# First gates inside the last FP4 products, a seven-product output gate for the first block, and weight sums on GpSimd

## The chip, the cores and the metric

The kernel runs on one core of a Trainium2 chip. The metric is its device time in microseconds; less is better. The core has TensorE (matrix products into PSUM, eight banks), VectorE and ScalarE (elementwise work from SBUF or PSUM), GpSimd (elementwise work from SBUF), SyncE (which issues most DMAs), and each of them works through its own instructions in order. Between engines an instruction waits on semaphores.

## The reference

Two layers over B = 2 sequences of T = 1024 tokens of C = 512 channels, all in float32: linear attention, a feed-forward part with FP4 weights, gated linear attention, and a feed-forward part over the 512 best-scored tokens of each sequence, each with a residual and a layer norm. The change lies at the seam of the second and third part:

```python
y = jnp.einsum('bsi,hi->bsh', h, w_down)                      # end of the FP4 part
y = y / jnp.sqrt(jnp.mean(y * y, axis=-1, keepdims=True) + EPS)
x = layernorm(x + y)
q = jax.nn.softmax(x @ Wq.T, axis=-1)                         # third part: 32 channels each
k = jax.nn.sigmoid(x @ Wk.T)
gf = jax.nn.log_sigmoid(-k)
o = _gla_chunk(q, k, x, gf)                                   # chunks of 64 tokens, decayed state
go = o @ Wog.T + x @ Wig.T                                    # the output gate, 512 x 512 each
on = o * lax.rsqrt(jnp.mean(o * o, axis=-1, keepdims=True) + EPS) * g_norm_w
x = layernorm(x + (on * (go * jax.nn.sigmoid(go))) @ Wo.T)
```

## The kernel before

The 2048 tokens are four blocks of 512; blocks 0 and 1 are the first sequence. The residual stream stays in SBUF (`x_t[blk]`, four tiles of 128 tokens), and its transpose is made on TensorE tile by tile (`turn`, L653, banks named `x2Tp`). A framework assigns the instructions to the engines, sets the waits, and orders each engine's stream; `tc.issue_after(ins)` puts what follows behind `ins` in the order. PSUM banks come in turn from two rings of four, `mm_bank` and `acc_bank`, and a product waits until the bank's last reader is done.

Many large products are made by seven block products instead of eight: sums of blocks of both operands, seven products of half size, and sums of the results.

- **FP4 down products** (`down`, L745 and L754): for each block P1, P2, P5, P4, P6, P7, P3, P8. Sums of their operands, `S` and `h`, are made on GpSimd (L760), the results are added into `y` on VectorE (L766 to L790). For the last block they run at the end of the stage in seven pieces, with the transposes of block 1 (`turn(1, ...)`) and the gate logits of the first sequence, `lp` (L661), between pieces. Then follow on ScalarE the squares of `y` (L823) and on GpSimd the inverse root (L827, L828); `Normed.rest` adds the scaled `y` to `x` on VectorE (L859) and normalises it.
- **`Gates`** (L993 to L1011) turns the logits of one sequence into q, k, l = log of the decay (through Exp and Ln on ScalarE and a reciprocal on VectorE), `ep` (one product with a triangle, L1008), e and kd. Before, it stands behind the FP4 stage.
- **`scores(blk)`** (L1025 to L1077): `cp` and exponentials of it, `tp`, then on VectorE last, km, kk, q4, qm, qk, qi; on TensorE `dp` (L1055), with `decay` copied from it; `sc`, `sk` and the states `up`. For block 0 it takes `fillers`, other work that is put between.
- **`attend(blk)`** (L1094, L1096): products into `op`, copied to `oT` on ScalarE, squares on ScalarE, and their sum `sum2` on GpSimd (L1103); `rms` (L1109) sums it over partitions with `mp`.
- **The output gate**: for blocks 1 to 3 `gate(blk)` (L1156), seven products of 8 matmuls with 256 columns, from sums of weights (`sums_of_gate`, gS1 to gS4 in `gsums`, VectorE, L974 to L977) and sums of x and o (`x_sum`, `o_sum`, `other_sums`, T1, T2, T4). For block 0 `plain_gate` (L1133, L1137): 16 matmuls of 512 columns with `Wig` and 16 with `Wog`, since the sums of weights come later.
- **`finish_by_seven(blk)`** (L1224): the last product with W1o, with sums from `sums_of_W1o` (VectorE, L1201) and `sums_of_u`.

The weights lie in four places, A0 to A3 (`place_w`); a new tenant waits for the last reader of the old one (`uT` takes the place of `y`). `w34` is a pool opened when the FP4 pool `fp4` is closed. `b2` and `rw`, 2 KB per partition each, serve as scratch until their own data is loaded; `rw` is first read at L1276, by the scores of the router for block 0.

Of the kernel before, what the change touches and what calls it, by code (L numbers as in the profile page):

```python
# [10 lines left out]
F32 = mybir.dt.float32  # L11
# [5 lines left out]
ALU = mybir.AluOpType  # L17
# [4 lines left out]
P = 128  # L22
# [51 lines left out]
def body(ctx: ExitStack, tc: tile.TileContext, a: dict, out: bass.AP):  # L74
# [594 lines left out]

    with tc.tile_pool(name="s2", bufs=1) as wk2:  # L670
# [137 lines left out]
        class Normed:  # L808
# [12 lines left out]
            def squares(self, part):  # L821
                for i in part:
                    nc.scalar.activation(junk, self.y[:, i], AF.Square, accum_out=self.ms[:, i : i + 1])  # L823

            def power(self):
                ms = self.ms
                nc.gpsimd.tensor_scalar(ms, ms, 1.0 / C, 1e-6, ALU.mult, ALU.add)  # L827
                nc.gpsimd.tensor_tensor(ms, ms, const("mhalf"), ALU.pow)  # L828
# [26 lines left out]
            def rest(self):  # L855

                for i in range(4):
                    x = x_t[self.blk][:, i]
                    nc.vector.scalar_tensor_tensor(x, self.y[:, i], self.ms[:, i : i + 1], x, ALU.mult, ALU.add)  # L859
                    row_stats(self.mv[:, i], x)  # L860
                    yield
                layernorm(x_t[self.blk], self.mv)
# [61 lines left out]
        for n, steps in enumerate((11, 12, 10, 12, 10, 10, 14)):  # L924
            with tc.issue_after(mm), tc.issue_after(hm):
                take(pieces, steps)
            if n < 2:
                turn(1, (2 * n, 2 * n + 1))
            if n == 2:
                lp = logits(0)  # L930
        now.squares(range(4))
        now.power()
# [8 lines left out]
    w1 = w34.tile([P, KC, DFF], F32, name="w1")  # L941
    nc.sync.dma_start(out=w1, in_=a["w1"].rearrange("(k p) f -> p k f", p=P))
    load_w(W1o, "W1oT")
    nc.sync.dma_start(out=rw, in_=a["rw"].to_broadcast([P, C]))
    nc.sync.dma_start(out=b2, in_=a["b2"].to_broadcast([P, C]))
    jk = ctx.enter_context(tc.tile_pool(name="jk", bufs=2))
    s3 = ctx.enter_context(ExitStack())
    wk = s3.enter_context(tc.tile_pool(name="s3", bufs=1))

    def part(i, shape, name):  # L950

        return w34.tile([P, *shape], F32, tag=f"B{i}", name=name)

# [12 lines left out]
    gsums = [part(i, [2, KC, 256], f"gsums{i}") for i in range(3)]  # L966
# [6 lines left out]
    def sums_of_gate():  # L973
        nc.vector.tensor_add(gS1, gA21, gA22)  # L974
        nc.vector.tensor_sub(gS2, gS1, gA11)
        nc.vector.tensor_sub(gS3, gA11, gA21)
        nc.vector.tensor_sub(gS4, gA12, gS2)  # L977
# [5 lines left out]

    class Gates:


        def __init__(self, lp):
            lg = lp.rearrange("p (i d) -> p i d", d=64)
            q, k, l, e = (wk.tile([P, 8, 32], F32, tag=n, name=n) for n in ("q3", "k3", "l3", "e3"))
            kd = wk.tile([P, 8, 4, 32], F32, tag="kd", name="kd")  # L990
            self.q, self.k, self.l, self.kd = q, k, l, kd

            nc.scalar.activation(k, lg[:, :, 32:], AF.Exp, scale=-1.0)  # L993
            nc.vector.tensor_scalar_add(k, k, 1.0)
            nc.vector.reciprocal(k, k)
            nc.scalar.activation(l, k, AF.Exp)
            nc.scalar.activation(l, l, AF.Ln, bias=const("one"))
            red = sp.tile([P, 8], F32, tag="red", name="red")
            nc.vector.tensor_reduce(red, lg[:, :, :32], AX.X, ALU.max)
            nc.vector.tensor_sub(q, lg[:, :, :32], red.unsqueeze(2).to_broadcast([P, 8, 32]))  # L1000
            nc.scalar.activation(q, q, AF.Exp)
            den = sp.tile([P, 8], F32, tag="den", name="den")
            nc.vector.tensor_reduce(den, q, AX.X, ALU.add)
            nc.vector.reciprocal(den, den)
            nc.vector.tensor_mul(q, q, den.unsqueeze(2).to_broadcast([P, 8, 32]))

            ep = mm_bank("ep")
            nc.tensor.matmul(ep[:, :256], const("suf"), l.rearrange("p i d -> p (i d)"), start=True, stop=True)  # L1008
            nc.scalar.activation(e.rearrange("p i d -> p (i d)"), ep[:, :256], AF.Exp)

            nc.vector.tensor_mul(  # L1011
                kd, e.unsqueeze(2).to_broadcast([P, 8, 4, 32]), k.unsqueeze(2).to_broadcast([P, 8, 4, 32])
            )

    def scores(blk, gates, beside=None):
# [12 lines left out]
        nc.scalar.activation(ex[:, 3], cp[:, :P], AF.Exp, scale=-1.0)  # L1028
# [96 lines left out]
    banks, last_3 = [], [None]  # L1125

    def plain_gate(m, first):

        cut = slice(m * P, (m + 1) * P)
        if first:  # L1130
            banks.append(acc_bank("go"))
            for k in range(KC):
                ins = nc.tensor.matmul(banks[m], Wig[:, k, cut], xT[0][:, k], start=k == 0, stop=False).ins  # L1133
            return ins
        else:
            for k in range(KC):
                nc.tensor.matmul(banks[m], Wog[:, k, cut], oT[0][:, k], start=False, stop=k == KC - 1)  # L1137
            if m == 0:
                uT[0] = place_w(3, "uT")
            sil = wk.tile([P, 512], F32, tag="sil", name="sil", bufs=2)  # L1140
            nc.scalar.activation(sil, banks[m], AF.Silu)
            nc.vector.scalar_tensor_tensor(uT[0][:, m], oT[0][:, m], gw[:, m : m + 1], sil, ALU.mult, ALU.mult)

    def gate(blk):


        u = uT[blk] = uT[0]
        c = u.rearrange("p (m e) (s t) -> p m e s t", e=2, s=2)
        c11, c12, c21, c22 = (c[:, :, e, s] for e in range(2) for s in range(2))
        x = xT[blk]  # L1150

        def product(ps, w, b, half, first):
            with tc.issue_after(last_3[0]):
                for m in range(2):
                    for k in range(KC):
                        ins = nc.tensor.matmul(  # L1156
                            ps[:, 256 * m : 256 * m + 256],
                            w[:, k, m],
                            b[:, k, 256 * half : 256 * half + 256],
                            start=first and m == 0 and k == 0,  # L1160
                            stop=k == KC - 1,
                            skip_group_check=True,
                        ).ins
            last_3[0] = ins
            return ps.rearrange("p (m t) -> p m t", m=2)
# [13 lines left out]
        nc.scalar.copy(c11, product(one, gA11, x, 0, True))  # L1179
        yield  # L1180
        p5 = product(two, gS1, T1, 0, True)
        yield
        nc.scalar.copy(c22, p5)
        yield
        nc.scalar.copy(c12, product(one, gS2, T2, 0, False))
        p2 = product(acc_bank("go"), gA12, oT[blk], 0, True)
        yield nc.vector.tensor_add(c11, c11, p2).ins
        p7 = product(one, gS3, x, 1, False)
        yield nc.vector.tensor_add(c22, c22, p7).ins
        nc.vector.tensor_add(c12, c12, product(two, gS4, oT[blk], 1, False))  # L1190
        yield end(0)
# [4 lines left out]
    def sums_of_W1o():  # L1196
        W1oT = part(3, [4, 512], "W1oT")
        B11, B12, B21, B22 = (W1o.rearrange("p (m e) (o c) -> p m e o c", e=2, o=2)[:, :, e, o] for e in range(2) for o in range(2))
        Ts = [W1oT[:, i].rearrange("p (m c) -> p m c", m=2) for i in range(4)]
        for dst, x, y in ((Ts[0], B12, B11), (Ts[1], B22, Ts[0]), (Ts[3], B21, Ts[1]), (Ts[2], B22, B12)):  # L1200
            nc.vector.tensor_sub(dst, x, y)  # L1201
        return (B11, B21, B22), Ts
# [369 lines left out]
    gates = Gates(lp)  # L1572

    def fillers(h):

        turn(2, (2 * h, 2 * h + 1))
        plain_gate(2 * h, True)
        return plain_gate(2 * h + 1, True)

    scored = scores(0, gates, fillers)  # L1580
    with tc.issue_after(scored):
        for _ in ending:
            pass
        sums_of_gate()
        x_sum(1)
    for blk in range(NB):
        if blk:
            if blk == 1:
                W1o_sums = sums_of_W1o()
            if blk < 3:  # L1590
                sums = sums_of_u()
        sum2 = attend(blk)
        if blk == 0:
            plain_gate(0, False)
        else:
# [13 lines left out]
            next(gating)  # L1609
# [3 lines left out]
        if blk == 1:  # L1613
            turn(3)
            gates = Gates(logits(1))
# [117 lines left out]
```

## Time and profile before

| | us |
|---|---|
| time, median of 3 runs (lowest to highest) | 985.53 (985.15 to 985.74) |
| the profiled execution: time | 985.74 |
| the profiled execution: span in the trace | 983.8 |
| TensorE clock granted, mean | 0.998 |
| last FP4 product P8 issued, first `go` with Wig begins | 551.65 |
| attend(0) begins | 575.77 |
| first product of `finish_by_seven` begins | 611.07 |

A profile line of a group gives line, engine, operation, output and inputs, how many, then busy time and the mean of one. PE is TensorE, DVE VectorE, ACT ScalarE, POOL GpSimd, SP SyncE. A float32 matmul shows as two records. In a timeline the first number is the start in us from the span's begin, the second the duration, and a bracket at the end is the idle time before it with what ended it. In a list of waits the numbers are the total, how many, and the longest.

### The profile page before, as it was taken

To read this page: it belongs to the slowest core of one execution; us is meant where nothing else is said; L and a number is where in the kernel's file an instruction comes from. 1 tells how busy PE (TensorE), PEld (TensorE's weight loads), DVE (VectorE), ACT (ScalarE), POOL (GpSimd) and SP (SyncE) were. 2 spreads that over 40 slices of the span, in tenths; PEclk is the share of its full clock that TensorE was granted. 3 is DMA by queue.
4 is the path that set the end of the run, shared out by engine and by line. 5 is a ranking of instruction groups with operands and counts; after the bars stand their busy time and mean duration, and the time that the engine had idled before them with its cause. 6 is when DMAs were issued, how large, how long until landed. Compare 5 with 4: busy or idle time off the path is not lost. (4 is left out here: it accounts for less than half of the span.)

```text
span 983.8 us, 11753 instructions
## 1 busy us (share of the span) xinstructions
PE 967.1 (98%) x4373; PEld 768.5 (78%) x4373; DVE 697.6 (71%) x1340; ACT 290.3 (30%) x496; POOL 302.9 (31%) x276
## 2 busy tenths in 40 slices
PE   9999999999999999999999999999999999999996
PEld 6668876785888888888889656979768588888885
DVE  3569986987975686686672566565897795789644
ACT  2344323333542272263240442132221123220000
POOL 1110282005887265575565022001032011000022
PEclk9999999999999999999999999999999999999999
DMA  9632222100000000000020500000004302140011
GB/s 333 194 88 74 87 69 64 49 1 1 1 1 1 1 1 1 1 11 1 0 86 1 224 1 1 1 1 1 1 33 139 128 17 70 44 171 1 1 43 43
DMA packets 25979, 48.85 MB, mean 50 GB/s; under 512 B 4684, under 2 KB 6732, under 8 KB 25411
## 3 DMA queue, kind: packets, MB, share of 16 engines
q1 hardware_dynamic: 23283, 42.98, 13.2%
q0 software_dynamic: 1920, 4.22, 1.1%
q10 hardware_dynamic: 720, 0.92, 0.3%
q8 instruction: 34, 0.56, 0.2%
q14 instruction: 22, 0.18, 0.1%
HBM read 39.70 MB, written 10.52 MB: 51 GB/s over the span
## 5 line engine op out<-in xcount | busy, mean ns | idle before, releaser
L181 POOL TENSOR_TENSOR rs<-rs,table 128x4 f32<-128x4 f32 (+1 forms) x21 | 20.3, 967 | 301.3 <-DVE rs L180 301.0
L709 DVE SCALAR_TENSOR_TENSOR gate<-gatep,scale,gate 128x512 f32<-128x512 f32 x123 | 91.5, 744 | 7.4 <-PE gatep L698 6.9
L709 DVE SCALAR_TENSOR_TENSOR up<-upp,scale,up 128x512 f32<-128x512 f32 x112 | 83.2, 743 | 0.2
L698 PE MATMUL gatep<-x1Th,wgu 128*128 128x512 f32 x176 | 73.1, 415 | 0.6 <-DVE x1Tl L212 0.6
L698 PE MATMUL upp<-x1Th,wgu 128*128 128x512 f32 x176 | 70.4, 400 | 0.1
L698 PE MATMUL gatep<-x1Tl,wgu 128*128 128x512 f32 x176 | 69.6, 395 | 0.0
L698 PE MATMUL upp<-x1Tl,wgu 128*128 128x512 f32 x176 | 69.5, 395 | 0.0
L703 ACT ACTIVATE gate<-gatep,scale 128x512 f32<-128x512 f32 x41 | 28.3, 690 | 112.1 <-PE gatep L698 105.7
L745 PE MATMUL P<-wdn,h 128*128 128x256 f32 x256 | 60.5, 379 | 0.0
L898 POOL TENSOR_TENSOR h<-up,gate 128x512 f32<-128x512 f32 x30 | 38.6, 1286 | 69.6 <-ACT gate L897 64.5
L745 PEld LDWEIGHTS P<-wdn,h 128*128 128x128 f32 x256 | 48.5, 190 | 6.7
L1103 POOL TENSOR_TENSOR sum<-sum,sq 128x512 f32<-128x512 f32 x12 | 18.0, 1499 | 101.6 <-issue 77.1
L367 PE MATMUL xk<-pair,x 128*128 128x512 f32 x96 | 42.7, 592 | 0.0
L188 DVE BATCH_NORM_STATS2 st<-x 128x6 f32<-128x512 f32 x64 | 41.9, 677 | 0.4
L698 PEld LDWEIGHTS upp<-x1Th,wgu 128*128 128x128 f32 x176 | 33.0, 188 | 10.6 <-DVE up L709 2.4
L698 PEld LDWEIGHTS gatep<-x1Th,wgu 128*128 128x128 f32 x176 | 33.1, 188 | 8.8 <-DVE gate L709 1.1
L698 PEld LDWEIGHTS upp<-x1Tl,wgu 128*128 128x128 f32 x176 | 33.1, 188 | 7.6 <-issue 0.2
L698 PEld LDWEIGHTS gatep<-x1Tl,wgu 128*128 128x128 f32 x176 | 33.1, 188 | 6.9
L1463 PE MATMUL yp<-w,h 128*128 128x256 f32 x168 | 37.7, 379 | 0.0
L745 PE MATMUL P<-T,S 128*128 128x256 f32 x160 | 35.8, 379 | 0.0
L1463 PEld LDWEIGHTS yp<-w,h 128*128 128x128 f32 x168 | 31.9, 190 | 4.3
L1377 ACT ACTIVATE h<-h,b 128x512 f32<-128x512 f32 x28 | 18.4, 713 | 57.2 <-DVE h L1401 34.6
(459 smaller groups left out, 2325.0 us busy)
## 6 DMA issues: line engine op xcount, KB each, us to landing
pk<-in_gu SPq DMA_DIRECT2D x16, 352.0 KB, 3.8
x<-in_x SPq DMA_DIRECT2D x4, 1024.0 KB, 13.1
w<-in_w SPq DMA_DIRECT2D x1, 4096.0 KB, 14.0
xs<-picked SPq DMA_DIRECT2D x4, 1024.0 KB, 5.1
out<-x SPq DMA_DIRECT2D x4, 1024.0 KB, 4.3
w<-in_w SPq DMA_DIRECT2D x4, 1024.0 KB, 7.0
x0T<-in_xT SPq DMA_DIRECT2D x3, 1024.0 KB, 7.1
pk<-in_dn SPq DMA_DIRECT2D x11, 256.0 KB, 3.4
```

What stands on the lines that cost most here:

```text
L181: power = nc.gpsimd.tensor_tensor(rs[:, :n], rs[:, :n], const("mhalf")[:, :n], ALU.pow).ins
L188: nc.vector.bn_stats(st, x)
L367: ins = nc.tensor.matmul(acc_of[b][c], x_t[blk][:, i, c * P : (c + 1) * P], pairs_of["k", blk][i // 2][:, i % 2], start=blk % 2 == 0 and i ...
L698: ins = nc.tensor.matmul(ps, wgu[:, k, at * P : (at + 1) * P], x[:, k], start=x is parts[0], stop=x is parts[1]).ins
L703: nc.scalar.activation(acc, ps, AF.Copy, scale=s)
L709: last = nc.vector.scalar_tensor_tensor(acc, ps, s, acc, ALU.mult, ALU.add).ins
L745: last_p[0] = nc.tensor.matmul(cut, x(j)[:, r], w[:, j], start=j == 0, stop=j == NP - 1 and tail is None).ins
L898: hm = nc.gpsimd.tensor_mul(h.chunk(f), up, gate).ins
L1103: nc.gpsimd.tensor_add(sum2, sum2, sq)
L1377: nc.scalar.activation(x, x, AF.Gelu_apprx_tanh, bias=b1[:, f : f + 1])
L1463: nc.tensor.matmul(ps[:, 256 * r : 256 * r + 256], x(r, j), w(j), start=j == 0, stop=j == NJ - 1)
```

## The change

- `Gates` moves ahead of the FP4 stage in the code and takes its rooms as an argument; its last step, kd, becomes `decayed`. The first sequence's gates are made behind `lp`, inside the last FP4 products, with q and k in `b2`, l and e in `rw`. The loads of `rw` and `b2` move behind the scores of block 1. For the second sequence it stands where it did.
- Block 0's output gate is made by `gate(0)`, in an order of products of its own; `plain_gate` goes. `x_sum(0)` and the first two products move in among the scores of block 0.
- `sums_of_gate` and `sums_of_W1o` are issued to GpSimd, the first right behind the FP4 stage, the second behind the inverse root of the last block's norm.
- The squares of the last block are issued behind the exponentials of block 0, into a scratch tile of their own, and its norm is split: the additions behind the scores of block 0, the statistics and the norm behind `other_sums(0)`.

```diff
@@ -667,6 +667,38 @@
+    class Gates:
+        def __init__(self, lp, rooms):
+            lg = lp.rearrange("p (i d) -> p i d", d=64)
+            self.q, self.k, self.l, self.e = q, k, l, e = rooms
...
+        def decayed(self, kd):
+            self.kd = kd
+            nc.vector.tensor_mul(
+                kd, self.e.unsqueeze(2).to_broadcast([P, 8, 4, 32]), self.k.unsqueeze(2).to_broadcast([P, 8, 4, 32])
+            )
@@ -857,8 +889,9 @@
                 nc.vector.scalar_tensor_tensor(x, self.y[:, i], self.ms[:, i : i + 1], x, ALU.mult, ALU.add)
-                    row_stats(self.mv[:, i], x)
-                    yield
+                yield
+                for i in range(4):
+                    row_stats(self.mv[:, i], x_t[self.blk][:, i])
                 layernorm(x_t[self.blk], self.mv)
@@ -927,9 +960,10 @@
             if n == 2:
-                lp = logits(0)
-        now.squares(range(4))
-        now.power()
+                gates = Gates(logits(0), [
+                    x[:, i * 256 : (i + 1) * 256].rearrange("p (i d) -> p i d", d=32) for x in (b2, rw) for i in range(2)
+                ])
         ending = now.rest()
@@ -938,18 +972,19 @@
+    gsums = [part(i, [2, KC, 256], f"gsums{i}") for i in range(3)]
+    W1oT = part(3, [4, 512], "W1oT")
     w1 = w34.tile([P, KC, DFF], F32, name="w1")
     nc.sync.dma_start(out=w1, in_=a["w1"].rearrange("(k p) f -> p k f", p=P))
     load_w(W1o, "W1oT")
-    nc.sync.dma_start(out=rw, in_=a["rw"].to_broadcast([P, C]))
-    nc.sync.dma_start(out=b2, in_=a["b2"].to_broadcast([P, C]))
@@ -971,47 +1005,16 @@
     def sums_of_gate():
-        nc.vector.tensor_add(gS1, gA21, gA22)
-        nc.vector.tensor_sub(gS2, gS1, gA11)
-        nc.vector.tensor_sub(gS3, gA11, gA21)
-        nc.vector.tensor_sub(gS4, gA12, gS2)
+        nc.gpsimd.tensor_add(gS1, gA21, gA22)
+        nc.gpsimd.tensor_sub(gS2, gS1, gA11)
+        nc.gpsimd.tensor_sub(gS3, gA11, gA21)
+        nc.gpsimd.tensor_sub(gS4, gA12, gS2)
@@ -1122,35 +1125,15 @@
-    def plain_gate(m, first):
...
     def gate(blk):
-        u = uT[blk] = uT[0]
...
         one, two = acc_bank("go"), acc_bank("go")
-        nc.scalar.copy(c11, product(one, gA11, x, 0, True))
+        p1 = product(one, gA11, x, 0, True)
         yield
         p5 = product(two, gS1, T1, 0, True)
         yield
+        if not uT:
+            uT[0] = place_w(3, "uT")
+        u = uT[blk] = uT[0]
...
+        nc.scalar.copy(c11, p1)
         nc.scalar.copy(c22, p5)
         yield
...
+        if blk == 0:
+            ins = p2()
+            p3 = p3()
+            nc.scalar.copy(c12, product(one, gS2, T2, 0, False))
+            yield ins
+            nc.vector.tensor_add(c12, c12, p3)
+            yield end(0)
+            yield p7()
+        else:
...
     def sums_of_W1o():
-        W1oT = part(3, [4, 512], "W1oT")
...
-            nc.vector.tensor_sub(dst, x, y)
+            nc.gpsimd.tensor_sub(dst, x, y)
@@ -1569,30 +1568,29 @@
-    gates = Gates(lp)
+    new_kd = lambda: wk.tile([P, 8, 4, 32], F32, tag="kd", name="kd")
+    gates.decayed(new_kd())
+    sums_of_gate()
+    x_sum(0)
+    gating = gate(0)
     def fillers(h):
         turn(2, (2 * h, 2 * h + 1))
-        plain_gate(2 * h, True)
-        return plain_gate(2 * h + 1, True)
+        next(gating)
+        return last_3[0]
     scored = scores(0, gates, fillers)
+    with tc.issue_after(last_ex[0]):
+        now.squares(range(4), jk.tile([P, C], F32, tag="junk", name="junk"))
+    powered = now.power()
     with tc.issue_after(scored):
-        for _ in ending:
-            pass
-        sums_of_gate()
-        x_sum(1)
+        next(ending)
     for blk in range(NB):
+        if blk == 1 or blk == 2:
+            sums = sums_of_u()
+        sum2 = attend(blk)
         if blk:
-            if blk == 1:
-                W1o_sums = sums_of_W1o()
-            if blk < 3:
-                sums = sums_of_u()
-        sum2 = attend(blk)
-        if blk == 0:
-            plain_gate(0, False)
-        else:
             o_sum(blk)
...
         if blk == 0:
-            for m in range(1, KC):
-                plain_gate(m, False)
-            continue
+            o_sum(0)
+            with tc.issue_after(powered):
+                W1o_sums = sums_of_W1o()
+            nc.sync.dma_start(out=rw, in_=a["rw"].to_broadcast([P, C]))
+            nc.sync.dma_start(out=b2, in_=a["b2"].to_broadcast([P, C]))
         other_sums(blk)
+        if blk == 0:
+            for _ in ending:
+                pass
```

More of the change, by code (lines that the diff above doesn't have):

```diff
@@ L668, in logits @@
         return lp
+    class Gates:
+        def __init__(self, lp, rooms):
+            lg = lp.rearrange("p (i d) -> p i d", d=64)
+            self.q, self.k, self.l, self.e = q, k, l, e = rooms
+            nc.scalar.activation(k, lg[:, :, 32:], AF.Exp, scale=-1.0)
+            nc.vector.tensor_scalar_add(k, k, 1.0)
+            nc.vector.reciprocal(k, k)
+            nc.scalar.activation(l, k, AF.Exp)
+            nc.scalar.activation(l, l, AF.Ln, bias=const("one"))
+            red = sp.tile([P, 8], F32, tag="red", name="red")
+            nc.vector.tensor_reduce(red, lg[:, :, :32], AX.X, ALU.max)
+            nc.vector.tensor_sub(q, lg[:, :, :32], red.unsqueeze(2).to_broadcast([P, 8, 32]))
+            nc.scalar.activation(q, q, AF.Exp)
+            den = sp.tile([P, 8], F32, tag="den", name="den")
+            nc.vector.tensor_reduce(den, q, AX.X, ALU.add)
+            nc.vector.reciprocal(den, den)
+            nc.vector.tensor_mul(q, q, den.unsqueeze(2).to_broadcast([P, 8, 32]))
+            ep = mm_bank("ep")
+            nc.tensor.matmul(ep[:, :256], const("suf"), l.rearrange("p i d -> p (i d)"), start=True, stop=True)
+            nc.scalar.activation(e.rearrange("p i d -> p (i d)"), ep[:, :256], AF.Exp)
+        def decayed(self, kd):
[3 more added lines that the diff above has]
+            )
     with tc.tile_pool(name="s2", bufs=1) as wk2:
@@ L819, in room, with squares @@
                 return [y[:, s, o] for s in range(2) for o in range(2)]
-            def squares(self, part):
+            def squares(self, part, junk=junk):
                 for i in part:
@@ L827, in power @@
                 nc.gpsimd.tensor_scalar(ms, ms, 1.0 / C, 1e-6, ALU.mult, ALU.add)
-                nc.gpsimd.tensor_tensor(ms, ms, const("mhalf"), ALU.pow)
+                return nc.gpsimd.tensor_tensor(ms, ms, const("mhalf"), ALU.pow).ins
             def scaled(self):
@@ L940, in body, with part @@
     w34 = ctx.enter_context(tc.tile_pool(name="w34", bufs=1))
+    def part(i, shape, name):
+        return w34.tile([P, *shape], F32, tag=f"B{i}", name=name)
+    gsums = [part(i, [2, KC, 256], f"gsums{i}") for i in range(3)]
+    W1oT = part(3, [4, 512], "W1oT")
     w1 = w34.tile([P, KC, DFF], F32, name="w1")
@@ L948, in body @@
     wk = s3.enter_context(tc.tile_pool(name="s3", bufs=1))
-    def part(i, shape, name):
-        return w34.tile([P, *shape], F32, tag=f"B{i}", name=name)
     NJ = NF // 2
@@ L965, in body @@
     )
-    gsums = [part(i, [2, KC, 256], f"gsums{i}") for i in range(3)]
     gS1, gS2, gS4 = (
@@ L982, in body @@
     oT, uT, tri, state, inv = {}, {}, {}, {}, {}
[L984 to L1013, printed above, removed]
     def scores(blk, gates, beside=None):
@@ L1027, in scores @@
         nc.scalar.activation(ex[:, :3].rearrange("p e t -> p (e t)"), cp, AF.Exp)
-        nc.scalar.activation(ex[:, 3], cp[:, :P], AF.Exp, scale=-1.0)
+        last_ex[0] = nc.scalar.activation(ex[:, 3], cp[:, :P], AF.Exp, scale=-1.0).ins
         tp = mm_bank("tp")
@@ L1123, in other_sums @@
         nc.vector.tensor_sub(T4, o[:, :, :256], T2)
-    banks, last_3 = [], [None]
-    def plain_gate(m, first):
[L1129 to L1134, printed above, removed]
-        else:
[L1136 to L1142, printed above, removed]
+    last_3, last_ex = [None], [None]
     def gate(blk):
-        u = uT[blk] = uT[0]
-        c = u.rearrange("p (m e) (s t) -> p m e s t", e=2, s=2)
-        c11, c12, c21, c22 = (c[:, :, e, s] for e in range(2) for s in range(2))
         x = xT[blk]
         def product(ps, w, b, half, first):
-            with tc.issue_after(last_3[0]):
+            with tc.issue_after(last_3[0]) if last_3[0] else contextlib.nullcontext():
                 for m in range(2):
@@ L1182, in gate @@
         yield
+        if not uT:
+            uT[0] = place_w(3, "uT")
+        u = uT[blk] = uT[0]
+        c = u.rearrange("p (m e) (s t) -> p m e s t", e=2, s=2)
+        c11, c12, c21, c22 = (c[:, :, e, s] for e in range(2) for s in range(2))
+        nc.scalar.copy(c11, p1)
         nc.scalar.copy(c22, p5)
         yield
[L1185 to L1191, printed above, removed]
+        p2 = lambda: nc.vector.tensor_add(c11, c11, product(acc_bank("go"), gA12, oT[blk], 0, True)).ins
+        p7 = lambda: nc.vector.tensor_add(c22, c22, product(one, gS3, x, 1, False)).ins
+        p3 = lambda: product(two, gS4, oT[blk], 1, False)
+        if blk == 0:
[7 more added lines that the diff above has]
+        else:
+            nc.scalar.copy(c12, product(one, gS2, T2, 0, False))
+            yield p2()
+            yield p7()
+            nc.vector.tensor_add(c12, c12, p3())
+            yield end(0)
         nc.scalar.activation(c21, product(one, gA22, T4, 0, False), AF.Silu)
@@ L1570, in finish_ffn @@
         next(two)
-    gates = Gates(lp)
+    new_kd = lambda: wk.tile([P, 8, 4, 32], F32, tag="kd", name="kd")
[3 more added lines that the diff above has]
+    gating = gate(0)
     def fillers(h):
         turn(2, (2 * h, 2 * h + 1))
-        plain_gate(2 * h, True)
-        return plain_gate(2 * h + 1, True)
+        next(gating)
+        return last_3[0]
     scored = scores(0, gates, fillers)
+    with tc.issue_after(last_ex[0]):
+        now.squares(range(4), jk.tile([P, C], F32, tag="junk", name="junk"))
+    powered = now.power()
     with tc.issue_after(scored):
-        for _ in ending:
-            pass
-        sums_of_gate()
-        x_sum(1)
+        next(ending)
     for blk in range(NB):
+        if blk == 1 or blk == 2:
+            sums = sums_of_u()
+        sum2 = attend(blk)
         if blk:
-            if blk == 1:
-                W1o_sums = sums_of_W1o()
-            if blk < 3:
-                sums = sums_of_u()
-        sum2 = attend(blk)
-        if blk == 0:
-            plain_gate(0, False)
-        else:
             o_sum(blk)
@@ L1608, in body @@
                     next(gating)
-            next(gating)
+        next(gating)
         if blk == 2:
@@ L1614, in body @@
             turn(3)
-            gates = Gates(logits(1))
+            gates = Gates(logits(1), [wk.tile([P, 8, 32], F32, tag=n, name=n) for n in ("q3", "k3", "l3", "e3")])
+            gates.decayed(new_kd())
         if blk < 3:
```

## The prediction

> **What bounds the kernel now.** I read four views, in this order. The page's first part says whether one engine fills the span:
>
> ```profile
> PE 967.1 (98%) x4373; PEld 768.5 (78%) x4373; DVE 697.6 (71%) x1340; ACT 290.3 (30%) x496; POOL 302.9 (31%) x276
> ```
>
> TensorE is without work for 983.8 - 967.1 = 16.7 us only, and most of that is the start and the tail behind the last matmul. So matmul time removed is time won, and each new gap on TensorE is time lost. The second view, the waits of TensorE from 500 to 680 us, lists the gaps where the change works (total us, times, longest):
>
> ```profile
> PE ep L1008 <- ACT l L997: 1.8, 2, 1.3
> PE dp L1055 <- DVE last L1040: 1.5, 2, 1.2
> PE x2Tp L197 <- ACT e L1009: 0.4, 1, 0.4
> PE mp L1109 <- POOL sum L1103: 0.3, 1, 0.3
> ```
>
> The third, the busy times from the first matmul behind the FP4 products (551.65) to the first product of `finish_by_seven` (611.07), which opens and closes the stretch that changes:
>
> ```profile
> 551.65:611.07 59.42, 56.34 (x246) 33.30 (x244) 40.10 (x71) 26.01 (x45) 11.21 (x9) 1.00 0.23 93
> ```
>
> Counted from issue to issue, the four gaps in it are 1.40 (`ep`), 0.51 (`x2Tp`), 0.45 (`mp`) and 1.31 (`dp`), 3.7 us; the rest, 55.7, is matmuls. The fourth view is the timeline, TensorE for prices and VectorE and GpSimd for what happens when both work (start, duration):
>
> ```profile
> 565.55 5.32 PE L1133 MATMUL go<-x2T,Wig 128*128 128x512 f32 x12
> 570.70 1.02 PE L1060 MATMUL sc<-qm,km 128*128 128x512 f32 x2
> ...
> 674.74 3.62 PE L1156 MATMUL go<-x2T,Wig 128*128 128x256 f32 x16
> 678.19 1.89 PE L1224 MATMUL grow<-W1oT,uS 128*128 128x256 f32 x8
> ...
> 580.25 1.55 POOL L1103 TENSOR_TENSOR sum<-sum,sq 128x512 f32<-128x512 f32 x1 [22.64 <-ACT sq L1102]
> 580.68 1.68 DVE L859 SCALAR_TENSOR_TENSOR x<-y,ms,x 128x512 f32<-128x512 f32 x1
> 583.56 2.30 POOL L1103 TENSOR_TENSOR sum<-sum,sq 128x512 f32<-128x512 f32 x1
> 583.56 1.19 DVE L974 TENSOR_TENSOR gsums<-Wig,Wog 128x1024 f32<-128x1024 f32 x1
> 584.76 2.19 DVE L1115 TENSOR_TENSOR gsums<-x2T 128x1024 f32<-128x1024 f32 x1
> 523.23 1.40 POOL L760 TENSOR_TENSOR S<-S,h 128x256 f32<-128x256 f32 x2 [2.59 <-PE P L745]
> ```
>
> An f32 matmul is two records. Of 512 columns it takes (570.70-565.55)/6 = 0.86 us, of 256 (678.19-674.74)/8 = 0.43. In the last six lines VectorE and GpSimd take turns: L859 alone takes 0.72 and here 1.68, since it stands until the GpSimd sum ends at 581.80; the GpSimd sum of 583.56 stands until L974 ends at 584.75; L1115 (1.2 alone) then stands until that sum ends at 585.86. It is one instruction of each, strictly in turn, and only for VectorE instructions with two SBUF inputs: the `y` additions, which read PSUM, keep their 0.69 while GpSimd runs (524.85).
>
> **What the Trainium skill says.** "GPSIMD Engine Reference", Specifications: GpSimd shares its SBUF interfaces with VectorE, with contention for VectorE instructions in a two-port mode or with two SBUF inputs. The trace agrees, and shows that the wait lasts for the other's whole instruction. The same page, section 3.1, gives 4497 ns for a GpSimd tensor_tensor of 2048 f32 elements; half is 2.25, an estimate. The trace has 0.72 for 256 elements and 1.27 for 512, which extends to 1.27 + 2*0.55 = 2.4 for 1024. "VectorE: DVE Perf Modes", the perf-mode tier table: f32 tensor_tensor runs at the lowest rate, 2293 ns for 2048; here 1.19 for 1024 agrees.
>
> **The change part by part.**
>
> *Seven products.* Out go 32 matmuls of 512 columns (27.5 us), in come 7*8 of 256 (24.2): -3.4 us, all on the path.
>
> *Gates early.* The chain `lp` to `l` ran beside nothing in the old place and cost the `ep` and `x2Tp` gaps. Now it starts when `lp` ends at 531.93, under P4. In the old place `l` was ready 5.28 us after its first activation began (553.75 to 559.03). Here that gives 537.3, and 0.3 more because k+1 meets a GpSimd sum of L760. `ep` stands behind one matmul of P6, at 537.40: a gap of 0.25 (0 to 0.7). The two old gaps go, -1.9. `rw` and `b2` as rooms move their loads behind `cp` and `tp` of block 1, some 581; L1276 reads `rw` at 637.7, so even the 10.2 us that the load took beside w1's is hidden. SP's queue has nothing behind them until the fetch of the routed rows. W1o and w1 are issued as before.
>
> *Sums on GpSimd.* This decides. In the built order the first sum, gS1, waits for the very last FP4 product, P8, because the rooms are freed as a pool. It can't run in GpSimd's idle time from 533.5 on. So four sums of 2.4 us start when VectorE's gate chain starts: kd, T1 (x_sum(0), moved ahead of `last`), last, km, kk, q4, qm, qk, qi, decay. Of these kd, T1, qm, qk and qi have two SBUF inputs. Take t=0 when P8 has been issued: 551.65 + 0.43 for `ep` + 0.25 = 552.33.
> - gS1 0.25 to 2.68; kd, ready at 0.85, stands, then 2.68 to 3.76.
> - gS2 3.76 to 6.04 (2.28 when it stood waiting); T1 6.04 to 7.12; gS3 7.12 to 9.40.
> - last to 7.3, km, kk, q4 to 8.1 (prices of 593.90 to 594.96); qm stands, 9.40 to 9.95; gS4 9.95 to 12.23; qk to 12.5; the 128x4 scaling of ms 0.15; qi to 13.2; decay 13.35.
>
> TensorE: cp 0.65, two tp 0.22, x2Tp 0.44, one go 0.43, x2Tp 0.44, seven go 3.02: 5.20. Then dp waits for `last` until 7.3, a gap of 2.1. dp, x2Tp, one go: 8.3. The last x2Tp takes dp's bank and waits for the copy `decay`: until 13.4, a gap of 5.1. Everything on TensorE is queued behind it. Without turns `decay` would be ready at 5.9 and both gaps nothing. If `last` takes a turn too, it is 14.4; with sums of 2.25 instead of 2.4, 12.9.
>
> *Behind it:* x2Tp 0.44, seven go 3.02, sc 0.95, sk 0.58, four up 3.54: attend(0) begins at 21.9 (its scores found VectorE free) and ends at 28.2 (6.25, as in 575.77 to 582.02). Squares are on ACT, 0.75 each, between x2T copies; hidden. The old 3.45 of Wog matmuls that covered the sums of squares are not there: cp 0.73, tp 0.22 and two go 0.86 reach 30.0, and then `mp` waits for the third sum on GpSimd. ACT has the third square at 29.6 as before plus two copies; GpSimd has first the second sum (28.5 to 29.8), then, new in between, the pow of the layer norm, which gives T2 on VectorE a turn (29.8 to 30.85) and takes 0.9, and then 1.2 for the third: 33.0. A gap of 3.0 (2.0 if T2 and pow fit in, 3.8 if the norm's statistics are late). ms3 stands ahead of km, kk, q4 on VectorE; q4 is at 35.1, `up` asks at 35.8. W1o's sums (4*1.27) run on GpSimd at 14 to 19, when VectorE has no two-input work. c11's copy waits for the last L859-like instruction on `y`, 25.9, and is asked at 26.3.
>
> *The rest to `finish_by_seven`:* mp 0.91, dp 0.21, three up with sc and sk 4.2, the six go left of the third product and 32 of the last four 16.4, attend(1) 7.15: 28.9. Work in all: 27.5 us other than the gate, 24.2 gate = 51.7. With gaps 2.1 + 5.1 + 3.0 the first `grow` is at 61.9, that is 614.2, against 611.07: +3.1. Check by differences: -3.4 work, -3.7 old gaps, +10.45 new gaps = +3.3. Behind it, the one-buffer oT of block 1 lands 2.4 us behind `grow`, T2 and the reads of `grow` are done at 66, the next product on that bank asks at 68.8: covered. From there on the order of TensorE is the same, so the difference stays.
>
> The profiled run took 985.74 for a span of 983.8, 1.9 around it; it was 0.2 above the median 985.53. A span of 986.9 makes 988.8 for that run and 988.6 for the median.
>
> **The rivals.**
> 1. *Forecast, turns at the port as in the trace*: +1.6 to +4.7 (the bounds above), 987.1 to 990.2. Chance 0.70.
> 2. *VectorE keeps its pace* (the other side: faster). The mechanism is the same port, at gS1 to gS4: if a GpSimd sum of 1024 lets VectorE in before it ends, the two gaps of 7.2 go, and the time is 985.5 + 3.1 - 7.2 = 981.4. It decides from the point where the turns cost less than 4.1 of the 7.2. For it: GpSimd's tensor_scalar at 119.23 (3.15 long) let one VectorE instruction through. Against: every tensor_tensor pair of the trace is exclusive. 0.11.
> 3. *Only one place bites*: the `mp` gap hides (sums in time), or the turns cost half. About +0.3, 985.8. For: each has a bound of its own. Against: GpSimd's order has pow ahead of the third sum. 0.13.
> 4. *A further gap*: silu of c11/c12 or c22's sum later than the 0.7 us to spare before the last gate product, or `mp` behind late statistics: 991 to 993. 0.06.
> That the change doesn't do what it says is excluded for the products; for the sums, "on GpSimd" doesn't mean beside the FP4 products, as said.
>
> **How the numbers follow.** The likeliest case gives 988.6. The range takes all of case 1 but its edge and most of 3: 985.0 to 990.4, leaving out 2, 4 and a little, 0.19. 0.2% is 2 us, about what a measurement of this kernel can tell from no change: slower is case 4 and nine tenths of case 1 and a little of 3, 0.71; within is the rest of 3 and the low edge of 1, 0.18; faster is 0.11.
>
> **What would show it.** In the new profile: gate work 3.4 shorter; no gap at `ep` over 0.7; kd and T1 above 2 us each in VectorE's rows and qm, qk, qi stretched; the last x2Tp of block 2 waiting some 5 us for `decay`; `dp` 2 for `last`; `mp` 3 for the GpSimd sum. Short kd and T1 rows beside running GpSimd sums would make the prediction wrong, and so would sums that start before P8 ends.

## The result, and the profile after

The changed kernel takes 994.75 us (median of six runs, 993.07 to 996.11) against 985.49 for the kernel before beside it (985.15 to 985.75): a ratio of 1.0092, 95% interval 1.0082 to 1.0102. It is slower by 9.3 us, where 3.1 were forecast, and outside the range. The profiled run took 994.78 for a span of 992.6.

The page of the changed kernel, the line of engine totals, and the row of the clock granted to TensorE in 40 slices (9 is 90% or more):

```profile
PE 970.6 (98%) x4421; PEld 782.5 (79%) x4421; DVE 703.4 (71%) x1339; ACT 288.5 (29%) x496; POOL 318.2 (32%) x284
...
PEclk9999999999999999999999789999999999999998
```

The same row of the kernel before:

```profile
PEclk9999999999999999999999999999999999999999
```

TensorE is busy 3.5 us longer than before, although 3.4 us of gate products went: some matmuls must have become slower. The clock rows say where. In the kernel before all slices have 9; here two slices have 7 and 8, some 545 to 595 us, just where the change is. (The 8 of the last slice lies behind the last matmul and slows nothing.) That row is in every page and was read too lightly.

The waits of TensorE from 500 to 680 us (total us, times, longest):

```profile
PE dp L1058 <- DVE last L1043: 4.2, 2, 3.9
PE mp L1112 <- POOL sum L1106: 3.0, 1, 3.0
PE x2Tp L197 <- DVE decay L1060: 1.4, 1, 1.4
PE ep L692 <- ACT l L681: 0.5, 1, 0.5
```

The forecast's four waits are there, in the places that it named. Next the timeline, TensorE first (start, duration), then VectorE and GpSimd:

```profile
554.62 3.19 PE L1139 MATMUL go<-x2T,Wig 128*128 128x256 f32 x14
561.72 0.59 PE L1058 MATMUL dp<-last,table 128*128 128x4 f32 x2 [3.91 <-DVE last L1043]
...
565.56 1.12 PE L197 MATMUL x2Tp<-table,x 128*128 128x128 f32 x4 [1.44 <-DVE decay L1060]
566.47 5.15 PE L1139 MATMUL go<-gsums,gsums 128*128 128x256 f32 x14
...
587.65 1.87 PE L1112 MATMUL mp<-table,sum 128*128 128x1 f32 x8 [2.99 <-POOL sum L1106]
...
619.92 1.89 PE L1223 MATMUL grow<-W1o,uT 128*128 128x256 f32 x8
...
553.25 2.89 DVE L698 TENSOR_TENSOR kd<-rw,b 128x1024 f32<-128x1024 f32 x1
556.07 3.37 DVE L1118 TENSOR_TENSOR gsums<-x2T 128x1024 f32<-128x1024 f32 x1
559.36 2.30 DVE L1043 TENSOR_SCALAR last<-table,ex 128x4 f32<-128x4 f32 x1
...
552.69 2.36 POOL L1008 TENSOR_TENSOR gsums<-Wig,Wog 128x1024 f32<-128x1024 f32 x1 [19.06 <-PE P L786]
555.13 3.22 POOL L1009 TENSOR_TENSOR gsums<-gsums,Wig 128x1024 f32<-128x1024 f32 x1
558.32 3.32 POOL L1010 TENSOR_TENSOR Wig<-Wig 128x1024 f32<-128x1024 f32 x1
...
584.44 1.92 POOL L181 TENSOR_TENSOR rs<-rs,table 128x4 f32<-128x4 f32 x1
586.35 1.25 POOL L1106 TENSOR_TENSOR sum<-sum,sq 128x512 f32<-128x512 f32 x1
```

The last two lines are the norm's power and the third sum of squares behind it, for which `mp` waits. Two more things are to be seen. VectorE and GpSimd alternate, each standing until the other's whole instruction is over, so that `last`, 128x4 elements, takes 2.30 us. And fourteen records of the same gate matmul take 3.19 us ahead of the first stop and 5.15 behind the stops. The busy times by stretch say what these have in common. Columns: length, then busy time of PE, PEld, DVE, ACT, POOL, the granted clock, DMA share, GB/s.

```profile
552.45:619.92 67.47, 59.12 (x292) 47.16 (x290) 41.35 (x62) 16.55 (x34) 24.43 (x15) 0.87 0.22 86
556.77:560.18 3.41, 1.03 (x5) 0.57 (x3) 3.41 (x2) 0.76 (x3) 3.41 (x2) 1.00 1.00 416
560.18:563.59 3.41, 1.87 (x8) 1.68 (x8) 3.38 (x5) 0.29 (x1) 3.41 (x2) 0.50 1.01 425
563.59:567.00 3.41, 1.97 (x8) 1.35 (x7) 1.91 (x4) 0.58 (x2) 3.24 (x5) 0.50 0.59 250
567.00:570.42 3.42, 3.42 (x10) 2.70 (x9) 0.00 (x0) 0.30 (x1) 3.34 (x3) 0.50 0.00 0
584.09:587.50 3.41, 0.57 (x3) 0.17 (x1) 1.54 (x3) 0.52 (x2) 3.31 (x3) 1.00 0.49 154
587.50:590.91 3.41, 3.26 (x13) 3.08 (x14) 1.16 (x5) 0.00 (x0) 1.12 (x2) 0.50 0.00 0
590.91:594.32 3.41, 3.41 (x8) 2.35 (x9) 1.62 (x4) 0.00 (x0) 0.00 (x0) 0.50 0.00 0
```

The clock is exactly halved, from 560.18 to 570.42 and from 587.50 to 594.32: three and two stretches of 3.41 us. 587.50 lies eight such stretches behind 560.18, so all changes stand on one grid. Each drop comes at the end of a stretch in which TensorE did little (1.03 and 0.57 us of 3.41).

I call this Theory A: a stop costs its own length and then the half clock behind it. The Trainium skill, "TensorE: Matmul & The Clock Gate", Part 1, states such a gate: TensorE falls to half its clock after an idle window of 3413 ns, is back after a busy one, and the window runs freely. The numbers agree with the length and with the half. They differ in one point: neither stretch ahead of a drop was wholly idle, so a stop shorter than the window is enough; here the measurement decides. The experiments set Theory A against two others. Theory B was that the matmuls are slow because of GpSimd's and VectorE's traffic at their shared port, and Theory C that the stops cost only themselves.

### The profile page after: what moved, and what is told of

The parts are those of the page before. It is cut to its first block, busy times and chain, and to the rows that moved or that the text cites. A ratio compares the mean times of both kernels' runs of the same rounds, so it can differ in the third digit from the quotient of the medians.

```text
span 992.6 us, 11851 instructions
## 1 busy us (share of the span) xinstructions
PE 970.6 (98%) x4421; PEld 782.5 (79%) x4421; DVE 703.4 (71%) x1339; ACT 288.5 (29%) x496; POOL 318.2 (32%) x284
```

## The experiments

**Stops without GpSimd (a single run, 1042.19 us against 985.84).** Artificial stops in the kernel before, in a stage where GpSimd's gate sums have no part:

```diff
+    def hold(n):
+        t = jk.tile([P, C], F32, tag="junk", name="hold")
+        nc.scalar.copy(t, last_ps[0])
+        for _ in range(n):
+            nc.scalar.copy(t, t)
+        spot = either_bank("hold")
+        with tc.issue_after(last_hp[0]):
+            held[0] = nc.tensor.matmul(spot[:, :4], ident, t[:, :4], start=True, stop=True).ins
...
     ins = nc.vector.tensor_sub(c21, c21, product(wA22, g, T4)).ins
+    hold(((0, 2, 4, 6), (3, 5, 8, 4))[b][g])
```

The next products are issued behind `held[0]`, so TensorE stands until the copies are done.

> The kernel before, with work added and none left out: behind each of the eight groups of the last layer's first weight, ScalarE copies one product's bank 1 + n times (about 0.55 us each) and a matmul of 4 columns waits for the last copy, so that TensorE stands still 0.9, 1.9, 2.9, 3.9 us in block 0 and 2.4, 3.4, 4.9, 2.9 us in block 1 (estimates). Neither GpSimd nor the port it shares with VectorE has a part in it. Theory A (long gaps halve TensorE's clock): gaps below about 2.5 us leave the clock of the windows at 1.00; those of 3.9 and 4.9 are followed by 3.4 to 7 us at 0.50, and so is 3.4 or 2.9 if it falls badly; the time grows by the gaps, some 23 us, plus 1.7 to 3.5 us for each that halves it, in all 29 to 37 us: 1015 to 1023. Theory B (traffic of GpSimd and the port made the matmuls slow): the clock stays at 1.00 behind every gap, and the time grows by the gaps alone, 1008.5.

The stops came out longer than estimated, 3.25 to 7.56 us (35.9 in all; the eighth was hidden), because the copies came late: the first stood until a subtraction on VectorE was done (793.77 us), and in the second group ScalarE's activations came between them. Each of the seven is followed by half clock: once 3.41 us, five times 6.83, once 10.24. The times by stretch around the first and second stop:

```profile
792.27:795.68 3.41, 1.19 (x6) 1.09 (x7) 3.41 (x8) 1.81 (x2) 0.00 (x0) 1.00 0.00 0
795.68:799.10 3.42, 3.42 (x10) 2.71 (x9) 3.42 (x10) 3.09 (x6) 0.00 (x0) 0.50 0.00 0
799.10:812.75 13.65, 9.66 (x45) 8.17 (x43) 12.76 (x35) 3.74 (x7) 5.04 (x5) 1.00 0.11 39
812.75:819.58 6.83, 6.45 (x16) 5.29 (x17) 0.00 (x0) 0.91 (x2) 3.19 (x4) 0.50 0.21 80
```

In the first pair GpSimd does nothing at all (POOL 0.00) and the clock is 0.50 all the same. Theory B has no place here; Theory C, which is 18 us short in the sum, has none either. The sum closes: 35.9 of stops; 47.8 us of half clock, of which in 11.3 TensorE still stood, so half of the rest, 18.2, lost; eight holding matmuls of some 0.3: 56.5, and 56.35 was measured.

**How short may a stop be (a single run each, 1035.79 and 999.68).** The same edit with the copies begun two products earlier, first with n from 6 to 10, then from 1 to 6:

> The kernel before with work added and none left out, as in the run with holds, but ScalarE's copies begin two products earlier, so that TensorE stands still for less: some 0.5, 1.1, 1.7 and 2.3 us in the four groups of block 0 and 1.1, 1.7, 2.3 and 2.9 in block 1 (estimates, from 0.62 a copy and 1.73 a product). So far a stop of 1.4 left the clock at 1.00 and one of 3.16, 2.3 of it within one stretch of 3.41 us between two possible changes of the clock, halved it. Theory A with a fixed grid of 3.41 us: stops up to 1.4 leave the clock; 2.9 halves it; of those between, the ones with most of their length within one stretch of the grid do, others don't, so equal stops can differ. Time 985.8 + 14 of stops + 2 for the holding matmuls + 1.7 or 3.4 for each that halves: 1003 to 1011. Theory F (each stop costs in proportion to its length): the half-clock time grows smoothly from the shortest stop on.

> The kernel before with work added and none left out: the run with short holds again with fewer copies, since the stops came out at 3.2 to 6.1 us there (3.24 for seven copies and 0.62 to 1.1 more for each further one). Expected stops: about 1.4, 2.0, 2.0 and once 2.6 us, one of some 3 in the first group. Theory A with a fixed grid of 3.41 us: those of 1.4 leave the clock at 1.00; of those of 2.0 and 2.6 some halve it for one stretch of 3.41 us (1.7 us lost each), depending on where they fall in the grid. Time 985.9 + 13 of stops + 2 + 2 to 7: 1003 to 1008. Theory F (in proportion to the length): every stop is followed by some half-clock time, shorter for shorter stops.

The first try missed its sizes: its stops were 3.22 to 6.14 us, and all seven halved the clock, the ones of 3.22 and 3.26 for one stretch, the others for two. The second has the short ones, shorter than estimated too (6.9 us in all where 13 were expected), so its time lies below its range of 1003 to 1008. Its times by stretch, around a stop of 0.52, one of 2.21 and one of 0.95:

```profile
791.43:800.00 8.57, 8.57 (x41) 7.59 (x42) 8.57 (x23) 4.28 (x6) 0.00 (x0) 1.00 0.00 0
803.85:806.21 2.36, 0.15 (x2) 0.00 (x1) 2.36 (x11) 2.21 (x4) 0.05 (x1) 1.00 0.01 3
806.88:810.30 3.42, 3.42 (x10) 2.70 (x9) 3.38 (x7) 1.82 (x3) 2.50 (x4) 0.50 0.21 77
...
821.43:829.00 7.57, 7.57 (x36) 6.72 (x37) 1.51 (x3) 2.38 (x4) 0.00 (x0) 1.00 0.17 48
```

Stops of 0.19, 0.52, 0.95 and 0.95 left the clock alone; 2.21 and 2.09 halved it for one stretch each, 1.7 us lost. So it is a step and not a share of the length, and Theory F is out.

**The stops filled (997.67, then 991.76 with a ratio of 1.0055, 1.0039 to 1.0072).** If the half clock comes from idleness, useless matmuls in the stops must make the kernel faster. The first try, four matmuls ahead of `dp` and three ahead of the last `x2Tp`:

```diff
+    def keep_busy(n, behind_):
+        with tc.issue_after(behind_):
+            for _ in range(n):
+                ins = nc.tensor.matmul(warm[0], ident, x_t[0][:, 0], start=True, stop=True).ins
+        return ins
...
+            return keep_busy(4, last_3[0])
...
+        turn(2, (2,))
+        with tc.issue_after(keep_busy(3, last_turned[0])):
+            turn(2, (3,))
```

> The kernel after with seven idle matmuls of 512 columns added, which nobody reads: four ahead of dp, three ahead of the last x2Tp, 6.0 us put into gaps of 4.1 and some 2.5. TensorE's order is otherwise that of the kernel after, and VectorE and GpSimd do the same. Theory A: the clock stays at 1.00 from 552 to 584, decay is as late as before, and what comes behind it runs at full rate, 2.4 us less: 992.4 (991.5 to 993.3), with more work. Theory B: the gates' products and x2Tp behind the gaps still take twice as long, 994.8 or a little above. What happens at mp stays as it is in both.

This took 997.67 (ratio 1.0120, 1.0104 to 1.0137). The first of the two `x2Tp` in this order is the one that takes dp's bank, so the three added matmuls came behind the wait for `decay` instead of into it; that stop (2.92 us) remained, the clock fell at 565.0 and the added work lay on the path. The second try gives dp's bank to the `x2Tp` that comes last:

```diff
+        banks = [mm_bank("x2Tp") for _ in range(2)]
+        turn(2, (3,), lambda _: banks[1])
+        with tc.issue_after(keep_busy(3, last_turned[0])):
+            turn(2, (2,), lambda _: banks[0])
```

> The kernel after with seven idle matmuls of 512 columns added, which nobody reads, now with the last three behind the x2Tp that doesn't wait for decay and ahead of the one that does. One gate product matmul comes behind decay that stood ahead of it. Theory A: the clock stays at 1.00 from 552 to 584, decay is ready as late as in the kernel after (13.1 us behind the last FP4 product), and sc is issued 17.0 us behind that product in place of 19.0: 2.0 less, 992.7 (992 to 993.6), although TensorE has 6.0 us more to do. Theory B: the matmuls behind decay still take twice as long: 994.8 to 995.5.

Its timeline of TensorE, and its time for the stretch of the first place:

```profile
557.63 3.60 PE L1597 MATMUL warm<-x,table 128*128 128x512 f32 x8
561.70 0.39 PE L1058 MATMUL dp<-last,table 128*128 128x4 f32 x2 [0.48 <-DVE last L1043]
...
565.55 0.66 PE L197 MATMUL x2Tp<-table,x 128*128 128x128 f32 x4 [0.39 <-DVE decay L1060]
566.04 3.62 PE L1139 MATMUL go<-gsums,gsums 128*128 128x256 f32 x16
569.50 1.02 PE L1063 MATMUL sc<-qm,km 128*128 128x512 f32 x2
```

```profile
551.50:584.00 32.50, 30.34 (x150) 21.12 (x148) 24.98 (x33) 11.18 (x26) 21.78 (x13) 1.00 0.43 171
```

`dp` and `x2Tp` are as late as in the changed kernel (9.27 and 13.1 us behind the last FP4 product), GpSimd and VectorE work as there, TensorE has 6 us more to do, and `sc` comes at 17.07 in place of 19.0: sixteen gate records take 3.62 where fourteen took 5.15. That is what Theory A says. The median of the four runs, 991.76, lies 0.24 us below its range and the profiled run, 992.95, inside it; all four lie below Theory B's 994.8.

**The second place (989.17, ratio 1.003, 1.0019 to 1.0040).** `mp` of block 0 issued later:

```diff
-        rms(blk, sum2)
+        if blk:
+            rms(blk, sum2)
+        else:
+            sum2_0 = sum2
...
         for n, done in enumerate(gating):
+            if blk == 0 and n == 0:
+                with tc.issue_after(last_3[0]), tc.issue_after(done):
+                    rms(0, sum2_0)
```

> The kernel after, with mp of block 0 issued behind the gate products that need oT, so that TensorE no longer stands 3 us for the third sum of squares. Theory A: the gap of 3.0 goes and with it the 3.4 us that 6.8 us at half clock cost, 994.75 - 6.4 = 988.3 (987.5 to 989.5). Theory C (the gap costs its own length only and the slow matmuls have another cause): 991.7. Theory D (this place is covered by something later, attend of block 1): 994 to 995.

5.6 us went, for a stop of 3.16 us. In the place of the second stop and its half clock the clock is now 1.00:

```profile
584.09:594.00 9.91, 9.22 (x35) 5.60 (x34) 9.88 (x18) 1.20 (x4) 4.09 (x3) 1.00 0.16 53
```

A stop of 0.69 at `dp` took part of the place. Theory C's 991.7 is out of the range of the runs (988.3 to 989.65).

**The first place: whose sums (986.48, ratio 1.0011, 1.0002 to 1.0020).** The gate's four sums back on VectorE, here the first, the others alike:

```diff
-        nc.gpsimd.tensor_add(gS1, gA21, gA22)
+        nc.vector.tensor_add(gS1, gA21, gA22)
```

> The kernel after, with the four sums of the gate's weights on VectorE in place of GpSimd and nothing else. VectorE has 4 x 1.2 more to do, but no turns; in TensorE's order 13 us of work now stand ahead of what waits for last and decay. Theory A (turns make the gaps, the gaps halve the clock): dp and x2Tp wait 0 to 1.5 us, no half clock there, mp's gap of 3 and its half clock stay: 994.75 - 4.1 - 1.4 - 3.6 + up to 1.5 = 985.7 to 987.2. Theory C: 989 to 990.5. Theory E (VectorE's whole chain is the limit, so the sums cost the same on either engine): 993 to 996.

8.3 us went, inside Theory A's 985.7 to 987.2. Giving VectorE 4.8 us more to do made it ready earlier: kd to gS4 run from 553.11 to 560.00 at 1.22 each, and `dp` waits 0.95, `x2Tp` not at all. The stop at `mp` remains, with one stretch of half clock behind it where the changed kernel has two and the expectation left both. So some 1.6 of the 8.3 us come from there and not from the edit's own place, and the hit is in that part luck; smaller stops at `up` and `sk` (0.70 and 0.17) took some of it back.

**Shorter turns (990.90, ratio 1.0044, 1.0028 to 1.0061).** The sums stay on GpSimd, each cut into four, again the first for all:

```diff
-        nc.gpsimd.tensor_add(gS1, gA21, gA22)
+        for k in range(KC):
+            nc.gpsimd.tensor_add(gS1[:, k], gA21[:, k], gA22[:, k])
```

> The kernel after with each of the four sums of the gate's weights on GpSimd cut into four instructions of 256 elements; nothing else. Theory A with turns of one instruction each: a VectorE instruction now waits 0.7 for its turn in place of 2.3, last is ready at 4.6 us behind the last FP4 product in place of 8.9, decay at 5.8 in place of 13.1, so TensorE (which asks at 5.2 and 6.3) stands at dp and x2Tp 0 to 1.0 in all, and the clock stays at 1.00 there: 994.75 - 4.1 - 1.4 - 3.6 + (0 to 1) = 985.7 to 986.7, mp's stop and its half clock still in it. Theory G (what VectorE loses depends on GpSimd's work as a whole, not on the length of its instructions): as after, 993 to 996.

The first place behaved as Theory A says: VectorE waits less, and the clock stays at 1.00 there. Its timeline on VectorE:

```profile
553.18 1.25 DVE L698 TENSOR_TENSOR kd<-rw,b 128x1024 f32<-128x1024 f32 x1
554.36 1.75 DVE L1122 TENSOR_TENSOR gsums<-x2T 128x1024 f32<-128x1024 f32 x1
556.03 0.69 DVE L1047 TENSOR_SCALAR last<-table,ex 128x4 f32<-128x4 f32 x1
...
570.90 5.42 DVE L891 SCALAR_TENSOR_TENSOR x<-y,ms,x 128x512 f32<-128x512 f32 x4
```

kd takes 1.25 in place of 2.89 and `last` 0.69 in place of 2.30. The miss of 4 us has two parts. My sum had `decay` ahead of qm, qk and qi on VectorE; in this kernel it comes behind them, at 560.54, so `x2Tp` still stood 1.96. And the turns moved on: W1o's sums on GpSimd now met the additions to x (L891, 5.42 for four, 2.73 in the run with sums on VectorE), which held back copies and squares on ScalarE; `tp` waited 2.1, `mp` 3.4, and the clock was halved for three stretches, 10.24 us.

**Both repairs (981.90, ratio 0.9958, 0.9942 to 0.9975; again 981.26, 0.9954, 0.9941 to 0.9968).** Sums on VectorE and `mp` late, the two edits above together:

> Both repairs: the four sums on VectorE, and mp of block 0 behind the gate products that need oT. Theory A, from the two single runs: 986.48 less mp's stop of 3.0 and the 1.7 to 3.4 of its half clock, plus 0 to 0.7 for dp of block 1: 980.1 to 982.5, faster than the kernel before by 3 to 5. If the two are not independent (VectorE late in both places): 984 to 986.

> The two repairs again (the four sums on VectorE, mp of block 0 late), beside the former kernel on one chip: 981.9 (981.5 to 982.5), with a spread below 1 us, since its longest stop is 0.95. Whichever of the two is lower, both stay below the kernel before by 3.5 to 6.

This version is faster than both kernels. Page and waits (500 to 680 us) of the second run:

```profile
PE 963.2 (98%) x4421; PEld 776.4 (79%) x4421; DVE 704.2 (72%) x1343; ACT 288.4 (29%) x496; POOL 308.6 (31%) x280
...
PEclk9999999999999999999999999999999999999998
```

```profile
PE dp L1058 <- DVE last L1043: 1.9, 3, 0.9
PE up L1075 <- DVE A L1067: 0.7, 1, 0.7
...
```

No stop is over 1 us, the clock row is all 9 but for the last slice, and TensorE is busy 3.9 us less than before: the 3.4 of the products that the change saves arrive at last. The second time lies 0.24 us below its expected range, and its spread of 1.2 us missed the 1 us expected.

**Split sums with the repairs (985.08, ratio 0.9991, 0.9984 to 0.9998; then 986.19, 1.0005, 0.9996 to 1.0013).** Two tries to keep the gate's sums on GpSimd, with `mp` late and W1o's sums moved. The second try also puts them behind the last of `other_sums(0)`, and takes a bank that nobody uses:

```diff
+            with tc.issue_after(normed), tc.issue_after(summed), tc.issue_after(last_sum[0]):
+                W1o_sums = sums_of_W1o()
...
+        if h:
+            mm_bank("spare")
```

> The split sums on GpSimd, with mp of block 0 behind the gate products that need oT, and with the sums of W1o on GpSimd behind the last sum of squares of block 0, so that they don't take turns with the additions to x. Theory A, from the run with split sums: 990.9 less 2.1 (tp's wait for squares that came late), 3.4 (mp's stop) and 5.1 (10.24 us at half clock), plus 0.7 for dp of block 1 and up to 1.5 for turns in the new place of W1o's sums: 980.3 to 982.5. If tp's wait has another cause than those turns: 982.4 to 984.6.

> The run with split sums and late mp, with its three remaining stops addressed: a bank left unused so that x2Tp doesn't wait for decay (a stop of 1.96, behind which the clock was halved for 3.41 us in that profile), and W1o's sums on GpSimd behind the last of the gate's input sums of block 0, so that qm, qk and qi of block 1 don't take turns with them (stops of 1.2 and 0.3 at up and sk). Theory A: 985.08 less 1.96, 1.7, 1.2 and 0.3 = 979.9 (979 to 981), and a narrow spread of the repeated times, as the kernel before has, since no stop over 1.4 us is left whose place in the grid could decide; the kernels with such stops spread by 1.8 to 3.8 us. If VectorE's chain ends as late without the decay wait (sc or the first up waits in its place): 982 to 983.5.

Both missed. In the first try the stop of 1.96 at `x2Tp`, harmless for the clock in the run with split sums, halved it for 3.41 us. Their times by stretch, one fence for each kernel, the run with split sums first:

```profile
556.56:559.97 3.41, 2.22 (x14) 1.69 (x12) 3.38 (x7) 1.50 (x5) 3.41 (x5) 1.00 1.02 411
559.97:563.38 3.41, 2.64 (x14) 2.40 (x15) 0.72 (x2) 0.59 (x1) 3.41 (x6) 1.00 1.01 428
```

```profile
557.78:561.19 3.41, 1.46 (x11) 1.05 (x9) 2.67 (x4) 0.58 (x1) 3.41 (x5) 1.00 0.97 406
561.19:564.60 3.41, 3.41 (x9) 2.70 (x9) 0.00 (x0) 0.58 (x1) 3.41 (x6) 0.50 1.01 430
```

An edge of the grid (559.97) cuts the same stop in two in one run and not in the other. W1o's sums then met qm, qk and qi of block 1 (stops of 1.17 and 0.31 at up and sk), which I had allowed for with up to 1.5. The rest of this miss is an error of the sum: the 5.1 us for 10.24 at half clock counted part of the stop at `mp` twice, since only 7.5 of the 10.24 were work, which makes 3.8. In the second try the first place is clean: `sc` 9.69 us behind the last FP4 product, against 13.56. But `issue_after` gives an order and no wait, W1o's sums began at 577.35, and there they met T2 and `last` of block 1:

```profile
577.60 2.28 DVE L1125 TENSOR_TENSOR gsums<-oT,gsums 128x1024 f32<-128x1024 f32 x1
579.80 1.22 DVE L1047 TENSOR_SCALAR last<-table,ex 128x4 f32<-128x4 f32 x1
```

This stop is the second miss: `dp` of block 1 stood 4.76 us and the clock was halved for 6.83. That try therefore doesn't test whether a kernel without such stops spreads less.

## Why the prediction was wrong

Its direction, its four places and their causes were right; the sum missed one term. By its own steps, from the last FP4 product's issue (552.45) to the first `grow` (619.92), 67.5 us where the prediction had 61.9:

- *The stops.* It had 2.1 (`dp`), 5.1 (`x2Tp`) and 3.0 (`mp`). Measured from issue to issue they are 4.08, 1.65 and 3.16. `last` did take a turn at the port, which the prediction had as its other bound, and so the wait moved from `x2Tp` to `dp`; `decay` released `x2Tp` at 13.1 us, 13.4 predicted. That these are so close is in part luck: `last` is missing in the prediction's list of instructions that take a turn, qk (0.41) stands in its sum for a turn that it didn't take, and the two misses cancel. With the short work between the two at full clock, the stop at `x2Tp` would have been 2.8, and the three 10.0 in all, against 10.2. The mechanism (whole turns at the port; the pow ahead of the third sum) and its size were right: the runs with VectorE's sums and with late `mp` took away what they should at the place that they changed, the run with split sums all but a stop of 1.96. That the third sum comes behind the pow is read from the timeline; no run changed that order.
- *The step that failed* is "With gaps 2.1 + 5.1 + 3.0 the first `grow` is at 61.9": each stop was counted at its own length, with all matmuls behind it at the prices of a trace without long stops. The term left out is the half clock. From 565.56 to 570.42 and from 587.65 to 594.32 it lost (4.86 + 6.67)/2 = 5.8 us, and 61.9 + 5.8 - 0.2 = 67.5. Filling the first place, moving the second, and stops in a kernel without the change show it. Between the matmuls of the kernel before no stop was over 1.40 and the clock stayed at 1.00, so no price of its trace held the term. But the trace held the sign: its last matmul ends at 975.4, and from 980.0 on the clock is 0.50, with nothing left to slow.
- *The products* were right: the work between the ends at full clock is 59.12 less half of the 13.93 us at half clock, 52.2, against 51.7. `ep` stood 0.5, inside its 0 to 0.7.
- *The rivals.* "VectorE keeps its pace" is refuted, kd and T1 at 2.89 and 3.37. "A further gap" came nearest in time (991 to 993) with the wrong mechanism. None had the clock, so the upper end of the range came from stops alone; bounding what a stop does to what follows would have carried it over 994.

## What to carry to other kernels

Price a stop of TensorE at its length only while it is short. Here 0.95 us cost itself and 2.1 us cost itself and 1.7 more; 3 to 5 us cost itself and 1.7 to 3.4 more, which is half of the work that fell into the one to three stretches at half clock. A row of the granted clock that leaves 9 is the first thing to look for when matmul time has risen without new matmuls.

When work goes to an engine that shares a port with the engine on the path, look at what its instructions meet, and not only at its idle time: a 128x4 instruction waited for a 128x1024 one. Shorter instructions shorten the turns; they don't remove them, and what was moved meets the next instruction down the line.

## What was not expected of the hardware

- The clock fell after stretches of 3.41 us with 0.57, 1.03, 1.19 and 1.46 us of work in them, and stayed at 1.00 after 2.22 and 2.64. Where between 1.46 and 2.22 the step lies wasn't tried.
- It came back only behind a stretch full of work: stretches with 2.83, 2.88 and 3.03 busy didn't bring it back in the run with holds. Nor did 587.50 to 590.91 in the changed kernel, 3.26 busy, with `mp`'s eight records of one column in it, nor, in the second run with filled stops, a stretch that was busy throughout but held the same `mp`:

```profile
585.92:589.33 3.41, 3.41 (x14) 3.14 (x14) 1.70 (x6) 0.00 (x0) 1.02 (x1) 0.50 0.00 0
```

Whether such matmuls count for less stays open.

- The turns of VectorE and GpSimd are not only for VectorE instructions with two inputs in SBUF, as the prediction read. In the changed kernel `rs` of the norm (L180, one input of 128x4) took 0.78 from 583.59, until a GpSimd sum ended at 584.34; in the kernel before, with GpSimd idle at 586.87, it took 0.16.
- A stop near 2 us is a matter of place in the grid. The changed kernel spread over 3.0 us and the first try with split sums over 3.4, where the run of both repairs with its short stops spread over 1.2. That the place differs from run to run would explain this. It was seen directly only between profiles of different kernels, but the mean clock of each run fits: of the twenty runs of the first try, the eight fastest (983.04 to 984.27) have 0.997 or 0.998, the six slowest (985.33 to 986.44) 0.995 or 0.996. An estimate from these: 0.002 of 985 us is 2 us of clock, near the 1.7 that one stretch costs. It stays an inference, since one run of each kernel was profiled.
